# Matrix loads, slots' state, temperature constants and a planner's ranks rearranged in a fused attention and slot-GRU block

## The chip, the cores and the metric

The kernel runs on one core of a Trainium2 chip. The core has a matrix engine (TensorE, PE in the profile; its weight loads are listed as PEld), a vector engine (VectorE, DVE), a scalar engine (ScalarE, ACT), GpSimd (POOL) and SyncE (SP), which here only issues DMAs. Each engine works through its own queue of instructions in order and waits on semaphores for the others. The metric is the device time of one execution in microseconds, the median of several. Before the change it is 694.39 us (three runs, 693.93 to 694.57).

## What is computed

The input x is 32 sequences of 512 tokens of 256 floats. Two pre-normed blocks are added to it. The first is a causal attention within each sequence of 512 tokens, whose keys and queries are the same 64 features; the second routes each token to 64 slots, lets a GRU update the slots of each sequence, and reads them back. Everything is float32. The reference, cut:

```python
# first block, on the layer-normed x
q = tanh(x @ W_charge.T + b_charge)[..., 0]
phi_c = mags * q[..., None] ** arange(5)
shell = x @ W_shell.T + b_shell
shell = shell / maximum(norm(shell), 1e-12)
proj = shell @ omega.T + rff_bias
phi_s = concatenate([cos(proj), sin(proj)], -1) * rff_scale
phi = (phi_c[..., :, None] * phi_s[..., None, :]).reshape(b, n, -1) @ W_combine.T
T = exp(-0.3 * abs(idx[:, None] - idx[None, :]) / 10.0)
temp = softplus(log_temp) + 0.1
logits = where(causal, einsum('bnd,bmd->bnm', phi, phi) * T / temp, -inf)
out = softmax(logits) @ (x @ W_v.T + b_v) @ W_out.T + b_out
# second block, on the layer-normed sum
S = broadcast(slot_init * slot_scale)
h = gelu(concatenate([x, mean(S)], -1) @ w1.T + b1)
route = (h @ w2.T + b2) / (abs(tau) + 0.1)
alpha = softmax over the 8 largest of 64, zero elsewhere
gi = einsum('bts,btd->bsd', alpha, x) / alpha.sum(1)
gx, gh = gi @ gru_wih.T + gru_bih, S @ gru_whh.T + gru_bhh
h_new = GRU(gx, gh, S)
out = einsum('bts,bsd->btd', alpha, h_new @ wv.T + bv) @ wo.T + bo
```

The layer norms have no weights, so the kernel folds them: a centred weight matrix and one scale for each token.

## The kernel before

**Groups and stages.** The 32 sequences are taken two at a time: 16 groups of 1024 tokens (eight tiles of 128). Each group goes through the same stages, which are also the names in the planner's table `DELAY`. *load*: x, twice (once as it is, once by blocks for VectorE's transposes, from group 2 on). *tokens*: transposes of x (`pta`, line 907, by TensorE for groups 0 and 1, by VectorE, line 929, later), statistics `bna` (800) and their scale `lna` on POOL (811 to 817), the projection `pf` (959) to 321 columns, that is value, shell and charge, and its eviction `sv` by VectorE (972). *angles*: norms (`sq`, `rn`, `shn`), transposes (`ptq` 1018, `pts` 1089), the product with omega (`pp` 1106), sines, and the powers `tp` (1152). *phi*: `pph` (1164), evicted at 1179. *weights*: logits `pl` (1221), mask and maximum (1250), exponential `pr` (1262). *values*: transposes of the weights (`ptp` 1299, `prT` 1317), the product `po` (1305) and the addition to x (1334). *normal*: second layer norm (`lnb`, `xm`). *router*: a turn of xm through DRAM (`xd`, `xmb`; the last group turns it on TensorE), the hidden layer `ph` (1431), `prr` (1454), its transposes `prt` (1460), the eight largest (1485, 1486) and the softmax (1494 to 1519). *taken*: slot input `psi` (1543). *gru*: `prz`, `pn` (1596), `rz` (1609) and the gates. *given*: slot values `pv` (1684), read back by `py` (1704), addition (1718) and store (1723).

**Who sets the order.** Nothing is emitted where it is written. Each piece is a step of a `Plan` with an engine, a cost in microseconds, what it must follow and which buffers it uses. `Plan.order()` gives every step that has no rank of its own the rank: group times `STRIDE`, plus a mix (weighted by `LATE`) of its earliest start and its latest start within its group, plus the stage's `DELAY`; the second number of a `DELAY` counts for the last groups. It then places steps one at a time by start time and rank, with `HOP` for a hand-over between engines, `TABLE` for ScalarE's change of function table and `SWITCH` as a handicap on a TensorE step of another tile shape. The steps are emitted in the order of placement, which fixes each engine's queue. Setup steps carry written ranks: the lower, the earlier. DMAs from SP and ACT, and apart from these the ones from POOL, take completion semaphores in turn, eight of each kind.

**The setup that the change touches.** `value_and_out` (413) folds W_v and W_out into the projection: it loads both, centres W_v on VectorE (432 to 435), multiplies (`pw` 446), copies the product into `wf` (460), multiplies the bias (`pb` 478) and adds it into `bias_f` (491). A second call does the same for wv and wo of the slots (`wov`, `bias_s`). `wf` is centred by a mean product (`pm` 519, subtraction 525), then written to DRAM and read back by blocks as `wfb` (533 to 550), which groups 2 and up use. POOL makes `di`, the table of token distances, by three iotas (602 to 604); VectorE casts it (609); from it come `dec_k` (exponential) and `dec_q`, its four reciprocals (643) scaled by the temperature (628). The temperature and tau go through `scalars_1` (absolute values, exponential), `scalars_2`, a logarithm and `scalars_3` (614 to 628). The slots' state `hs` is loaded twice (for the two sequences of a group) with its scale `sc` (702 to 706) and multiplied. `whh` and the loads behind it feed the GRU's constant half (`pgh`, 744 to 780).

Scratch tiles of the setup stand in the five buffers of x: `setup_0` holds W_v and W_out, `setup_1` whh, `setup_2` wv and wo. Group 2's x takes the buffer of `setup_0` once the setup is done with it.

Of the kernel before, what the change touches and what calls it, by code (L numbers as in the profile page):

```python
# [11 lines left out]
AF = mybir.ActivationFunctionType  # L12
# [59 lines left out]
}  # L72


HOP = 0.21
TABLE = 1.28
SWITCH = 4.13
STRIDE = 29.1
LATE = 0.69

DELAY = {
    "setup": (0.0, 0.0),
    "load": (-39.8, 3.7),
    "tokens": (0.2, -3.0),
    "angles": (-18.5, -12.2),
    "phi": (8.4, 6.8),
    "weights": (14.1, -12.0),
    "values": (5.1, -15.9),
    "normal": (-0.8, 5.2),
    "router": (-1.4, -7.2),  # L90
    "taken": (1.6, -23.5),
    "gru": (16.3, 6.1),
    "given": (-12.8, -6.4),
}

SPARE = 3
# [149 lines left out]
def block_kernel(ctx: ExitStack, tc: tile.TileContext, a: dict, out: bass.AP):  # L246
# [163 lines left out]
        load("ACT", wf[:, :, 0:SHELL], rows(a["W_shell_t"]), 64, rank=-42.0, land=4.0),  # L410
    ]

    def value_and_out(wv_ap, bv_ap, wo_t_ap, bo_ap, w_dst, b_dst, n, centred, engs, rank):

        at = 2 * n
        wv = part(at, 0, [P, KD, D])
        wo_t = part(at, KD * D, [P, KD, D])
        bv_rep = part(at, 2 * KD * D, [P, KD, P])
        bo = part(at, 2 * KD * D + KD * P, [P, D])
        of = wv.of  # L420
        bv = const(f"bv{n}", [P, KD])
        mean = const(f"wv_mean{n}", [P, KD])
        land = 3.5 if centred else None
        l_wv = load(engs[0], wv, rows(wv_ap), 256, rank=rank, land=land)
        l_wo = load(engs[1], wo_t, rows(wo_t_ap), 256, rank=rank, land=land)
        l_bv = load(engs[2], bv, bv_ap.rearrange("(k p) -> p k", p=P), 8, rank=rank)
        l_bo = load(engs[2], bo, bo_ap.partition_broadcast(P), 128, rank=rank)
        last = l_wv
        if centred:

            def centre():
                nc.vector.tensor_reduce(mean, wv(), AX.X, ALU.add)
                nc.vector.tensor_scalar(mean, mean, 1.0 / D, None, ALU.mult)
                for k in range(KD):
                    nc.vector.tensor_scalar(
                        wv()[:, k, :], wv()[:, k, :], mean[:, k : k + 1], None, ALU.subtract
                    )

            last = add("DVE", 1.6, centre, [l_wv], of, rank=rank)
        done, made = [], []  # L440
        for m in range(KD):
            pw = bank(f"pw{n}_{m}")

            def project(m=m, pw=pw):
                for k in range(KD):
                    nc.tensor.matmul(
                        pw()[:, 0:D],
                        wv()[:, k, m * P : (m + 1) * P],
                        wo_t()[:, k, :],
                        start=(k == 0),  # L450
                        stop=(k == KD - 1),
                    )
# [13 lines left out]

        def spread():
            for k in range(KD):
                nc.vector.tensor_scalar(
                    bv_rep()[:, k, :], onesP, bv[:, k : k + 1], None, ALU.mult  # L470
                )

        s = add("DVE", 0.5, spread, [l_bv, s_ones], of, rank=rank)
        pb = bank(f"pb{n}")

        def project_bias():
            for k in range(KD):
                nc.tensor.matmul(
                    pb()[:, 0:D],
                    bv_rep()[:, k, :],  # L480
                    wo_t()[:, k, :],
                    start=(k == 0),
                    stop=(k == KD - 1),
                )

        s = add("PE", 1.6, project_bias, [s, l_wo], [pb] + of, rank=rank)
        done.append(
            add(
                "DVE",
                0.42,  # L490
                lambda: nc.vector.tensor_tensor(b_dst, pb()[:, 0:D], bo(), ALU.add),
                [s, l_bo],
                [pb] + of,
                rank=rank,
            )
        )
        return done, made
# [7 lines left out]
        bias_f[:, C_V:NF],  # L505
        0,
        True,
        ("SP", "ACT", "POOL"),
        -40.0,
    )  # L510
    l_bsh = [
# [21 lines left out]
    for q in range(P // SQ):  # L533
        for k in range(KD):
            kd, lo = divmod(q * KD * SQ + k * SQ, P)
            W_PFB.append(
                load(
                    "SP",
                    wfb[q * SQ : (q + 1) * SQ, k, :],
                    wf[lo : lo + SQ, kd, :],  # L540
                    40,
                    W_PF,
                    rank=2.0,
                    land=4.0,
                )
            )
# [66 lines left out]
    def scalars_1():  # L613
        nc.scalar.activation(sa, lt, AF.Abs)
        nc.scalar.activation(tau, tau, AF.Abs)
        nc.scalar.activation(sa, sa, AF.Exp, scale=-1.0)
        nc.scalar.activation(dec_k, df(), AF.Exp, scale=DECAY)

    def scalars_2():
        nc.vector.tensor_scalar(sa, sa, 1.0, None, ALU.add)  # L620
# [6 lines left out]
        nc.vector.reciprocal(rtemp, sb)  # L627
        nc.vector.tensor_scalar(dec_q, dec_q, rtemp, -1.0, ALU.mult, ALU.mult)

    s = add("ACT", 1.4, scalars_1, [l_lt, l_tau, s_df], df.of, table="exp", rank=4.0)  # L630
    s_exp = s
    s = add("DVE", 0.6, scalars_2, [s], rank=5.0)
    s_tau = s
    s = add("ACT", 1.5, lambda: nc.scalar.activation(sa, sa, AF.Ln), [s], table="ln", rank=5.0)
    s_sb = s

    def decays(after):

# [4 lines left out]
                lambda c=c: nc.vector.reciprocal(  # L643
                    dec_q[:, c * P : (c + 1) * P], dec_k[:, c * P : (c + 1) * P]
                ),
                [s_exp] + after,
                rank=9.0,
            )
            for c in range(NT)
        ]  # L650
        s_dec.append(add("DVE", 1.0, scalars_3, [s_sb] + s_rec, rank=10.0))

    s_dec = []


    def make_mask():
# [45 lines left out]
    l_hs = []  # L702
    for bb in range(GB):
        r = slice(bb * SLOTS, (bb + 1) * SLOTS)
        l_hs.append(load("SP", hs[r, :], a["slot_init"], 64, rank=31.0))
        l_hs.append(load("SP", sc[r, :], a["slot_scale"], 1, rank=31.0))
    s_hs = add(
        "DVE", 0.35, lambda: nc.vector.tensor_scalar(hs, hs, sc, None, ALU.mult), l_hs, rank=40.0
    )
# [33 lines left out]

    whh = part(1, 0, [P, KD, 3 * D])
    bih_rz = part(1, KD * 3 * D, [P, 2 * D])
    l_whh = load("SP", whh, rows(a["gru_whh_t"]), 768, rank=50.0)
    l_bih = [
        load("SP", bih_rz, a["gru_bih"][0 : 2 * D].partition_broadcast(P), 256, rank=51.0),
        load("SP", bih_n, a["gru_bih"][2 * D : 3 * D].partition_broadcast(P), 128, rank=51.0),
# [3 lines left out]
    for lo, n in ((0, 2 * D), (2 * D, D)):  # L753
# [26 lines left out]
        s = add("PE", 2 * n / 300.0, hidden, [s_hst, l_whh], [pg] + hs_t.of + whh.of, rank=70.0)  # L780
        W_GRU.append(add("DVE", 1.3, hidden_bias, [s, l_bhh] + l_bih, [pg, bhh] + whh.of, rank=71.0))
    s_wov, _ = value_and_out(
        a["wv"], a["bv"], a["wo_t"], a["bo"], wov, bias_s, 1, False, ("SP",) * 3, 72.0
    )


# [560 lines left out]
    def router(g, s_x, ln):  # L1347
# [134 lines left out]
        for t in range(GT):  # L1482
# [18 lines left out]
            "ACT",  # L1501
            0.68,
            lambda: nc.scalar.activation(rl(), rl(), AF.Exp, scale=rtau),
            [s, s_tau],
            [rl],
            "exp",
        )
# [225 lines left out]
    for g in range(NG):  # L1733
        plan.group = g
        plan.stage = "load"
        if g:

            if g == 1:
                load_x(g, rank=-30.0, lands=(8.5, 9.5))
            elif g == 2:  # L1740
                load_x(g, rank=0.0, lands=(6.0, 7.0))
            else:
                load_x(g, [l_w1s, l_whh])
        sv, s_sv, phi, s_phi = features(g)
# [66 lines left out]
```

## Time and profile before

The profiled execution took 696.3 us; the profile's span is 694.5 us, so 1.8 us lie around it. The mean granted clock of TensorE is 0.990 of full speed.

| | us | what it is |
|---|---|---|
| median of three runs | 694.39 | 693.93 to 694.57 |
| profiled execution | 696.3 | span 694.5 |
| first TensorE matmul (`pw`) | 10.78 | |
| first projection (`pf` of group 0) | 17.90 | TensorE was busy for 6.62 us until 17.40 |
| weights of group 0 (`pl`) | 48.95 | |
| projection of group 2 | 68.84 | |
| one group in the middle | 39.9 | `pf` of successive groups at 265.10, 305.00, 344.90, 384.80 |
| last `po` | ends near 641 | |
| last store | 694.5 | |

Times are read from the timeline of the trace. A group's "busy" is the time in which an engine runs an instruction; waits on semaphores are not in it. Where a row of the profile ends in brackets, it gives the idle time of the engine just before, and what ended it.

### The profile page before, as it was taken

To read this page: it belongs to the slowest core of one execution; us is meant where nothing else is said; L and a number is where in the kernel's file an instruction comes from. 1 tells how busy PE (TensorE), PEld (TensorE's weight loads), DVE (VectorE), ACT (ScalarE), POOL (GpSimd) and SP (SyncE) were. 2 spreads that over 40 slices of the span, in tenths; PEclk is the share of its full clock that TensorE was granted. 3 is DMA by queue.
4 is the path that set the end of the run, shared out by engine and by line. 5 is a ranking of instruction groups with operands and counts; after the bars stand their busy time and mean duration, and the time that the engine had idled before them with its cause. 6 is when DMAs were issued, how large, how long until landed. Compare 5 with 4: busy or idle time off the path is not lost.

```text
span 694.5 us, 12285 instructions
## 1 busy us (share of the span) xinstructions
PE 664.7 (96%) x3946; PEld 457.7 (66%) x3946; DVE 581.4 (84%) x1812; ACT 454.2 (65%) x1064; POOL 214.0 (31%) x400
## 2 busy tenths in 40 slices
PE   3979999999999999999999999999999999999885
PEld 3747666667666666767666666666766676678453
DVE  3987878799898989989897988989898968878586
ACT  1446676848585866758495775758676677486731
POOL 3550524133150613324061422406151233212200
PEclk9999999999999999999999999999999999999989
DMA  6672732445544444444535353543543433301004
GB/s 179 165 204 68 205 100 73 111 141 130 154 115 130 150 114 161 101 143 128 175 93 149 125 122 135 139 152 96 148 132 82 161 82 87 97 1 62 0 13 170
DMA packets 174255, 83.25 MB, mean 120 GB/s; under 512 B 123664, under 2 KB 173392, under 8 KB 174192
## 3 DMA queue, kind: packets, MB, share of 16 engines
q1 hardware_dynamic: 172880, 81.95, 41.8%
q8 instruction: 31, 0.51, 0.3%
q10 hardware_dynamic: 1104, 0.36, 0.2%
q0 software_dynamic: 208, 0.17, 0.2%
q14 instruction: 32, 0.26, 0.1%
HBM read 50.67 MB, written 31.46 MB: 118 GB/s over the span
## 4 chain that ended last, share of the span: by engine, by line
PE 89%; DVE 4%; DMA 2%; ACT 2%; issue 1%; POOL 0%; ACTq 0%; DVEq 0%; SPq 0%
PE po L1305 20%; PE pf L959 19%; PE ph L1431 7%; PE pl L1221 5%; PE pph L1164 5%; PE ptp L1299 5%; PE psi L1543 5%; PE py L1704 4%; PE prz L1596 4%; PE pn L1596 2%; PE pv L1684 2%; PE prr L1454 2%; PE pta L1667 1%; PE pp L1106 1%; DMA setup<-in_W_out_t_dram 1%; DMA wih<-in_gru_wih_t_dram 1%
## 5 line engine op out<-in xcount | busy, mean ns | idle before, releaser
L1305 PE MATMUL po<-sv,prT 128*128 128x256 f32 x640 | 151.7, 381 | 0.8 <-ACT prT L1317 0.8
L1305 PEld LDWEIGHTS po<-sv,prT 128*128 128x128 f32 x640 | 115.5, 189 | 24.2 <-issue 8.6
L959 PE MATMUL pf<-wfb,xT 128*128 128x321 f32 x448 | 125.6, 436 | 0.0
L959 PEld LDWEIGHTS pf<-wfb,xT 128*128 128x128 f32 x448 | 83.5, 189 | 39.7 <-DVE top L1485 3.5
L1371 ACT ACTIVATE xm<-x,lnb 128x256 f32<-128x256 f32 x128 | 63.9, 502 | 61.7 <-POOL lnb L1359 61.6
L1359 POOL TENSOR_SCALAR lnb<-lnb 128x2 f32<-128x2 f32 (+1 forms) x48 | 20.8, 434 | 266.7 <-DVE x L1334 264.4
L1334 DVE SCALAR_TENSOR_TENSOR x<-po,den,x 128x256 f32<-128x256 f32 x128 | 57.9, 479 | 27.1 <-PE po L1305 26.6
L1262 ACT ACTIVATE pr<-lg,nm 128x512 f32<-128x512 f32 (+3 forms) x128 | 70.8, 557 | 4.9 <-DVE nm L1250 4.0
L972 DVE SCALAR_TENSOR_TENSOR sv<-pf,lna,bias_f 128x321 f32<-128x321 f32 x128 | 64.7, 537 | 5.7 <-PE pf L959 5.1
L1401 ACT ACTIVATE xm<-x,lnb 128x256 f32<-128x256 f32 x112 | 56.9, 589 | 7.8 <-POOL lnb L1387 7.8
L1250 DVE CUSTOM_DVE_ANT_0 lg<-pl,mask 128x512 f32<-128x512 f32 (+3 forms) x128 | 55.6, 479 | 1.6 <-PE pl L1221 1.3
L1718 DVE TENSOR_TENSOR x<-py,x 128x512 f32<-128x512 f32 x64 | 39.8, 683 | 17.4 <-PE py L1704 17.3
L1431 PE MATMUL ph<-xmT,w1b 128*128 128x512 f32 x112 | 52.7, 594 | 0.0
L1317 ACT COPY prT<-ptp 128x384 f32<-128x384 f32 (+1 forms) x96 | 46.1, 516 | 5.4 <-PE ptp L1299 5.2
L800 DVE BATCH_NORM_STATS2 bna<-x 128x6 f32<-128x256 f32 x128 | 49.4, 413 | 0.0
L1299 PE MATMUL ptp<-ident,pr 128*128 128x128 f32 x320 | 45.8, 275 | 0.0
L1221 PE MATMUL pl<-phi 64*128 64x256 f32 (+1 forms) x384 | 43.8, 358 | 0.2 <-DVE phi L1179 0.2
L1299 PEld LDWEIGHTS ptp<-ident,pr 128*128 128x128 f32 x320 | 36.5, 141 | 9.3 <-issue 6.8
L1164 PE MATMUL pph<-tp,wc 64*64 64x256 f32 x640 | 39.8, 392 | 0.8 <-DVE tp L1152 0.8
L1152 DVE TENSOR_TENSOR tp<-tp,qs 128x1024 f32<-128x1024 f32 x32 | 38.7, 1211 | 2.1 <-ACT tp L1138 1.9
L1221 PEld LDWEIGHTS pl<-phi 64*128 64x128 f32 x384 | 30.5, 186 | 11.1 <-issue 7.2
L929 DVE STREAM_TRANSPOSE xT<-xb 128x512 f32<-128x512 f32 x56 | 36.6, 685 | 0.0
(174 smaller groups left out, 1241.6 us busy)
## 6 DMA issues: line engine op xcount, KB each, us to landing
x<-in_x_dram SPq DMA_DIRECT2D x32, 512.0 KB, 4.6
out_dram<-x SPq DMA_DIRECT2D x64, 256.0 KB, 2.5
xb<-in_x_dram SPq DMA_DIRECT2D x112, 128.0 KB, 2.8
xd<-xm SPq DMA_DIRECT2D x28, 512.0 KB, 2.9
xmb<-xd SPq DMA_DIRECT2D x112, 128.0 KB, 2.7
setup<-in_gru_whh_t_dram SPq DMA_DIRECT2D x1, 768.0 KB, 4.6
wih<-in_gru_wih_t_dram SPq DMA_DIRECT2D x1, 768.0 KB, 10.6
wfb<-wf SPq DMA_DIRECT2D x8, 40.1 KB, 3.4
```

The costliest lines, as they stand in the source:

```text
L959: nc.tensor.matmul(pf()[:, 0:NF], tile_()[:, k, c * P : (c + 1) * P], w[:, k, :], start=(k == 0), stop=(k == KD - 1),)
L972: lambda t=t, pf=pf: nc.vector.scalar_tensor_tensor(sv()[:, t, :], pf()[:, 0:NF], ln()[:, 1, t : t + 1], bias_f, ALU.mult, ALU.add,),
L1164: nc.tensor.matmul(phs[h]()[bb * COMB : (bb + 1) * COMB, 0:HT], wc[r, m, :], tp()[r, m, bb * HT : (bb + 1) * HT], start=(m == 0), stop=(m ...
L1221: nc.tensor.matmul(pls[bb]()[:, off[i] + lo : off[i] + lo + w], phi()[r, 0, q : q + P], phi()[r, 1, k : k + w], start=True, stop=True,)
L1250: nc.vector.tensor_tensor_reduce(out=lg()[:, c], in0=pls[bb]()[:, c], in1=mask[:, T - w : T], scale=1.0, scalar=TOP, op0=ALU.add, op1=ALU.min,
L1262: nc.scalar.activation(pr()[:, c], lg()[:, c], AF.Exp, bias=nm(), scale=-1.0, accum_out=den()[:, tiles.index(i), bb : bb + 1],)
L1299: nc.tensor.transpose(pt()[:, j : j + P], prs[bb]()[:, j : j + P], ident)
L1305: nc.tensor.matmul(po()[:, d * D : (d + 1) * D], pr_t()[:, lo : lo + P], sv()[:, bb * NT + j, C_V:NF], start=(j == 0), stop=(j == i),)
L1334: nc.vector.scalar_tensor_tensor(xt()[:, t, :], po()[:, d * D : (d + 1) * D], den()[:, d, bb : bb + 1], xt()[:, t, :], ALU.mult, ALU.add, ...
L1371: lambda bb=bb, i=i: nc.scalar.activation(xm()[:, bb * NT + i, 0:D], xt()[:, bb * NT + i, :], AF.Square, bias=ln()[:, 2, bb, i : i + 1], a ...
L1401: nc.scalar.activation(xm()[:, t, 0:D], xt()[:, t, :], AF.Identity, bias=bias, scale=scale)
L1431: nc.tensor.matmul(ph(), w1[:, k, :], dst()[:, k, :], start=(k == 0), stop=(k == KD - 1))
```

## The change

1. **Planner numbers.** `HOP` 0.21 to 0.29, `SWITCH` 4.13 to 0, `STRIDE` 29.1 to 22.7, `LATE` 0.69 to 0.98, and every `DELAY` but that of the setup. The order of all groups' steps on every engine is computed anew.
2. **W_out.** Its load goes from ACT's queue to SP's, right behind W_v. `value_and_out` takes a rank for the two matrices apart from that of their biases.
3. **Slots' state.** The four loads of `hs` and `sc` go from SP's queue to POOL's, behind those of bv, b_out and omega and ahead of the iotas.
4. **GRU and value matrices.** `whh`, `wv` and `wo` are issued on SP ahead of group 2's tokens, `wfb` and group 2's x later than before.
5. **Temperatures.** `scalars_1` no longer contains the exponential of `dec_k`, which stays early; the rest, with `scalars_2`, the logarithm and `scalars_3`, follows group 0's evictions.
6. **Reciprocals.** Each of the four reciprocals of `dec_k` follows one of group 0's last four evictions, instead of all four following all evictions.

```diff
-HOP = 0.21
+HOP = 0.29
-SWITCH = 4.13
-STRIDE = 29.1
-LATE = 0.69
+SWITCH = 0.0
+STRIDE = 22.7
+LATE = 0.98
-    "load": (-39.8, 3.7),
-    "tokens": (0.2, -3.0),
-    "angles": (-18.5, -12.2),
-    "phi": (8.4, 6.8),
-    "weights": (14.1, -12.0),
-    "values": (5.1, -15.9),
-    "normal": (-0.8, 5.2),
-    "router": (-1.4, -7.2),
-    "taken": (1.6, -23.5),
-    "gru": (16.3, 6.1),
-    "given": (-12.8, -6.4),
+    "load": (4.8, -12.9),
+    "tokens": (8.2, 7.0),
+    "angles": (-54.3, -7.8),
+    "phi": (-1.8, -10.7),
+    "weights": (11.9, 26.1),
+    "values": (9.7, -3.6),
+    "normal": (11.8, 2.3),
+    "router": (10.9, -19.7),
+    "taken": (-37.2, -20.0),
+    "gru": (-2.4, -1.6),
+    "given": (-3.5, 15.0),
...
-        land = 3.5 if centred else None
-        l_wv = load(engs[0], wv, rows(wv_ap), 256, rank=rank, land=land)
-        l_wo = load(engs[1], wo_t, rows(wo_t_ap), 256, rank=rank, land=land)
+        land = 3.3 if centred else None
+        first = rank if first is None else first
+        l_wv = load(engs[0], wv, rows(wv_ap), 256, rank=first, land=land)
+        l_wo = load(engs[1], wo_t, rows(wo_t_ap), 256, rank=first, land=land)
...
-        ("SP", "ACT", "POOL"),
+        ("SP", "SP", "POOL"),
...
-                    rank=2.0,
+                    rank=22.0,
...
-        nc.scalar.activation(dec_k, df(), AF.Exp, scale=DECAY)
...
-    s = add("ACT", 1.4, scalars_1, [l_lt, l_tau, s_df], df.of, table="exp", rank=4.0)
-    s_exp = s
-    s = add("DVE", 0.6, scalars_2, [s], rank=5.0)
-    s_tau = s
-    s = add("ACT", 1.5, lambda: nc.scalar.activation(sa, sa, AF.Ln), [s], table="ln", rank=5.0)
-    s_sb = s
+    s_exp = add(
+        "ACT",
+        0.7,
+        lambda: nc.scalar.activation(dec_k, df(), AF.Exp, scale=DECAY),
+        [s_df],
+        df.of,
+        table="exp",
+        rank=4.0,
+    )
...
-                [s_exp] + after,
-                rank=9.0,
+                [s_exp, after[4 + c]],
+                rank=-1.0,
...
-        s_dec.append(add("DVE", 1.0, scalars_3, [s_sb] + s_rec, rank=10.0))
+        s = add("ACT", 0.7, scalars_1, [l_lt, l_tau] + after, table="exp", rank=10.0)
+        s = add("DVE", 0.6, scalars_2, [s], rank=10.0)
+        s_tau.append(s)
+        s = add("ACT", 0.3, lambda: nc.scalar.activation(sa, sa, AF.Ln), [s], table="ln", rank=10.0)
+        s_dec.append(add("DVE", 1.0, scalars_3, [s] + s_rec, rank=10.0))
...
-        l_hs.append(load("SP", hs[r, :], a["slot_init"], 64, rank=31.0))
-        l_hs.append(load("SP", sc[r, :], a["slot_scale"], 1, rank=31.0))
+        l_hs.append(load("POOL", hs[r, :], a["slot_init"], 64, rank=-14.0))
+        l_hs.append(load("POOL", sc[r, :], a["slot_scale"], 1, rank=-14.0))
...
-    l_whh = load("SP", whh, rows(a["gru_whh_t"]), 768, rank=50.0)
+    l_whh = load("SP", whh, rows(a["gru_whh_t"]), 768, rank=-10.0)
...
-        a["wv"], a["bv"], a["wo_t"], a["bo"], wov, bias_s, 1, False, ("SP",) * 3, 72.0
+        a["wv"], a["bv"], a["wo_t"], a["bo"], wov, bias_s, 1, False, ("SP",) * 3, 72.0, -9.0
...
-                load_x(g, rank=0.0, lands=(6.0, 7.0))
+                load_x(g, rank=20.0, lands=(6.0, 7.0))
```

More of the change, by code (lines that the diff above doesn't have):

```diff
@@ L411, in block_kernel, with value_and_out @@
     ]
-    def value_and_out(wv_ap, bv_ap, wo_t_ap, bo_ap, w_dst, b_dst, n, centred, engs, rank):
+    def value_and_out(
+        wv_ap, bv_ap, wo_t_ap, bo_ap, w_dst, b_dst, n, centred, engs, rank, first=None
+    ):
         at = 2 * n
@@ L650, in decays @@
         ]
-        s_dec.append(add("DVE", 1.0, scalars_3, [s_sb] + s_rec, rank=10.0))
-    s_dec = []
+        s = add("ACT", 0.7, scalars_1, [l_lt, l_tau] + after, table="exp", rank=10.0)
[3 more added lines that the diff above has]
+        s_dec.append(add("DVE", 1.0, scalars_3, [s] + s_rec, rank=10.0))
+    s_dec, s_tau = [], []
     def make_mask():
@@ L1503, in router @@
             lambda: nc.scalar.activation(rl(), rl(), AF.Exp, scale=rtau),
-            [s, s_tau],
+            [s] + s_tau,
             [rl],
```

## The prediction

> **What bounds the kernel now.** I read the page's busy table first, then the slices, then the table by stretches, because a mean hides the ends.
>
> ```profile
> PE 664.7 (96%) x3946; PEld 457.7 (66%) x3946; DVE 581.4 (84%) x1812; ACT 454.2 (65%) x1064; POOL 214.0 (31%) x400
> ...
> PE   3979999999999999999999999999999999999885
> ...
> PE 89%; DVE 4%; DMA 2%; ACT 2%; issue 1%; POOL 0%; ACTq 0%; DVEq 0%; SPq 0%
> ```
>
> TensorE is busy 664.7 of 694.5 us and carries 89% of the chain that ended last. Outside the first and last slices there is nothing to win except by giving TensorE less to do. The stretches say the same in microseconds (columns: stretch, its length, then each engine's busy time, granted clock, DMA share, GB/s):
>
> ```profile
> 0.00:17.40 17.40, 6.62 (x28) 5.70 (x29) 6.44 (x19) 1.90 (x3) 6.88 (x22) 1.00 0.66 178
> 17.40:34.70 17.30, 17.30 (x82) 12.83 (x80) 16.08 (x47) 8.34 (x16) 9.74 (x22) 1.00 0.64 165
> 34.70:52.00 17.30, 13.14 (x109) 8.23 (x108) 15.46 (x35) 8.09 (x13) 8.84 (x15) 0.90 0.79 204
> ...
> 69.00:104.00 35.00, 33.63 (x197) 23.69 (x196) 28.91 (x83) 24.45 (x62) 13.02 (x29) 1.00 0.55 151
> 104.00:138.00 34.00, 33.11 (x176) 22.49 (x177) 27.01 (x90) 25.23 (x57) 9.34 (x15) 1.00 0.36 94
> ...
> 277.00:312.00 35.00, 35.00 (x212) 24.34 (x209) 30.55 (x98) 24.02 (x58) 11.25 (x20) 1.00 0.46 124
> ...
> 642.00:660.00 18.00, 15.95 (x59) 7.54 (x56) 9.17 (x37) 13.82 (x27) 3.90 (x6) 1.00 0.00 0
> 660.00:677.00 17.00, 15.08 (x79) 9.28 (x80) 13.88 (x48) 4.93 (x12) 0.00 (x0) 0.80 0.03 10
> 677.00:694.50 17.50, 9.34 (x52) 5.91 (x50) 10.71 (x22) 2.22 (x5) 0.00 (x0) 0.91 0.50 172
> ```
>
> TensorE's idle time is 10.8 us in the first stretch, 4.2 at 34.7 to 52, 2.3 from 69 to 138, none in the middle (35.00 of 35.00), and 2.1 + 1.9 + 8.2 in the tail. At 34.7 to 52 the clock is 0.90 too: it was halved from 42.77 to 46.20, after a thin stretch. The first wait, by the view of waits (total, times, longest):
>
> ```profile
> PE pw L446 <- DMA setup<-in_W_out_t_dram: 10.8, 1, 10.8
> ```
>
> The transfers of the start, by the view of DMA issues (the last column is us from issue to landing):
>
> ```profile
> setup<-in_W_v_dram SPq DMA_DIRECT2D x1, 256.0 KB, 3.5
> setup<-in_W_out_t_dram ACTq DMA_DIRECT2D x1, 256.0 KB, 8.9
> ...
> setup<-in_b_out_dram POOLq DMA_DIRECT2D x1, 128.0 KB, 7.9
> ...
> hs<-in_slot_init_dram SPq DMA_DIRECT2D x2, 64.0 KB, 2.4
> ...
> om<-in_omega_t_dram POOLq DMA_DIRECT2D x4, 8.0 KB, 8.0
> ```
>
> The same 256 KB took 3.5 us as the first on SP and 8.9 us on ACT's queue.
>
> **W_out on SP: what the first wait is worth.** Behind W_v (issued 0.73, landed 4.28) W_out should land near 5.5. VectorE centres W_v until 6.37, so pw can start at about 6.5 instead of 10.78. pw and pb take 5.3 us cold (3.75 + 1.5), so they end near 11.8. If nothing else held it, pf_0 (17.90, that is 7.1 us after pw) would start near 13.6: a gain of 4.3.
>
> **Slots' state on POOL's queue: what is late next.** POOL already issues bv, b_out and four om, by 5.24. Four more make ten, and in the changed kernel's built order the ninth and tenth carry a wait on the semaphores of bv and b_out: they are issued only when those have landed. b_out landed at 10.43. Behind those issues POOL has the three iotas of di (5.2 to 6.6 now, 2.1 us with gaps). So di would be ready at 10.4 + 2 = 12.4, and VectorE's cast of di stands ahead of both copies of pw in VectorE's order. It now comes early, by the timeline:
>
> ```profile
> 8.46 0.42 DVE L609 CAST setup<-di 128x512 f32<-128x512 int32 x1
> ```
>
> The copies, three statistics and bias_f behind it take about 3 us, to 15.8. Then come hs's scaling and only then wf's centring, which pf_0 needs; hs's scaling waits for the four landings. TensorE has pt_hs ahead of the second half of group 0's transposes, so it waits too.
>
> Here a rule stands against a row. The Trainium skill, "DMA: Bandwidth & Descriptors", section "Anatomy of one DMA — SWDGE (gpsimd) path", prices a transfer from GpSimd's queue at about 2.0 us plus its bytes at 436 KB/us, an estimate of 2.15 us for 64 KB and 2.3 for b_out. By it b_out lands at 4.9, nobody waits, di is ready near 8.5 and the gain is the 4.3. The rows say 7.9 for b_out and 8.0 for om at 8 KB, while the loads of x run. I take the row: hs issued near 8.5 and sc near 10.5 land at 14.8 to 16.5, wf is centred at about 16.6, and pf_0 starts at 17.4 (16.3 to 19). **Gain 0.5** (between -1.1 and 4.3). TensorE then has about 3 us of idling after pb, as long as the half-clock stretch that the trace shows at 42.77 to 46.20; one such stretch at half speed over the transposes costs **+0.8** (0 to 1.7).
>
> **GRU and value matrices ahead of x_2; wfb and x_2 late.** 768 + 512 KB go first. At the 165 to 204 GB/s of those stretches that is some 7 us of transfer, of which 2 to 3 delay xb_2 (to about 30); VectorE comes to group 2's transposes near 38. Hidden; if it were not, 2 us. In return pgh (1.9 + 0.9 us), pb1 (0.6) and pw1 (1.6) can stand in the gaps between group 0's angles and its weights. By pl_0 the changed order has done 3.7 us more (these, less pts_1 and pp_1), and at pf_2, which now starts at 68.84, 2.84 more. TensorE is idle 4.2 us at 34.7 to 52, but VectorE has 15.46 of 17.30 there and gets 1.65 us more ahead of phi_0. So about 3.0 of the idling is filled: **-3.0** (-3.5 to +1), of which 0.4 is given back in the stretch up to 69: **+0.4**.
>
> **Reciprocals and temperatures.** The four reciprocals (3.38 us in one piece at 27.23) go between the evictions of group 0: the same work. The last eviction is about 1.1 us later, and rn_0, which stood behind the four, is not. scalars_1 leaves dec_k's exponential and goes behind all evictions; scalars_2 and 3 with it. They are 0.14 to 0.5 us each. Rates for weights are needed only at pl_0 (48.95), and the chain Abs, Exp, Ln, reciprocal, scaling is 3 to 4 us with table loads of 1.28. Nothing, in the shadow of the angles; without it 1.3 for a table load.
>
> **New ranks.** HOP, SWITCH, STRIDE, LATE and all delays change, so the whole order changes. From 69 to 138 the angles get more room (ptq_1 had a wait of 2.56 for POOL's qrep, pts_2 0.94, ptq_2 0.89): 2.3 us were lost there and I take **-1.2** (-2.3 to 0). In the middle TensorE is full and can only lose. Before, groups 4 to 12 repeat one order; in the changed kernel each group's differs. Some producers stand closer to their users: pt_gi of group 11 has 0.3 us of other matmuls ahead of prz where VectorE or ScalarE must copy between them, pts_9 0.4, pv of groups 4 and 12 0.8 instead of 1.8, pph 1.3 to 2.3 ahead of pl instead of 8.8. No row shows those waits. Near rows are the short waits of 0.3 to 0.9 in the ramp; six to eight places lose part of that: **+1.0** (0 to 6).
>
> Matmuls of another tile shape follow each other more often: 215 changes of shape against 204. From the trace, a matmul of 256 columns starts 215 ns after one of the same shape and 306 to 309 ns after a change, so a change is worth 92 ns: 11 x 0.092 = **+1.0**. The Trainium skill, "TensorEngine Tiling (Array Packing)", section "Key Properties", says a mode switch drains the array; with the constant part of an isolated matmul from "TensorE: Matmul & The Clock Gate", "Single matmul latency", some 166 ns warm, it would be an estimate of 1.8. I take the row.
>
> **Tail.** In the changed order 3.2 us more of TensorE's work (prz_13, pn_13, pt_hn_13, one ptb_14) stands ahead of the last po_15, which ended near 641: **+3.2** at that point, and less is left behind it. What is left ran with waits:
>
> ```profile
> 657.69 1.28 ACT L1503 ACT_TABLE_LOAD   x1 [0.41 <-DVE rl L1494]
> ...
> 660.33 0.92 PE L1460 MATMUL prt<-ident,rlT 128*128 128x128 f32 x4 [2.23 <-ACT rlT L1468]
> ```
>
> prt_15 waits for ScalarE, which loaded a table for group 14's exponential first; with prt_14 ahead of the third transpose instead of behind it, that moves 0.65 earlier. py_13 (673.76 and 675.19) and VectorE's four adds of x_13 (674.93 to 677.65, ahead of rh at 677.56) stood between psi_15 and rz_15, and go in front: 1.7 to 1.9. Together **-2.5** (-4 to 0).
>
> **The sum**, against the profiled execution: -0.5 + 0.8 - 3.0 + 0.4 - 1.2 + 1.0 + 1.0 + 3.2 - 2.5 = -0.8. The profiled execution took 696.3 (span 694.5 and 1.8 around it); the median of the runs shown is 694.39, so I set the difference against that: **693.5 us**.
>
> **Rivals.** A, the start's gain is real: POOL's transfers are quicker when W_out no longer shares the time, or the semaphores do not hold di. For it: 2.4 us for the same hs on SP. Against: 6.4 to 8.0 for bv and om, the small transfers of POOL's queue. Then -4.3 in place of -0.5 + 0.8, partly absorbed by VectorE: about 689.5.
>
> B, slower: the irregular order stalls a full TensorE. Place: groups 3 to 13, at edges with less than about 1 us of other matmuls between a producer on TensorE and its next user. Price: a round trip by ScalarE or VectorE takes 1 to 2 us (copy 0.5 to 0.7 and two hand-overs), so 0.6 us a group, 11 groups, +6.6 in place of +1.0: about 699. It decides from 0.3 us a group on. For it: VectorE has 30.55 of 35.00 there, so it runs late easily. Against: only a few edges are that tight.
>
> C: the ramp gives nothing, since VectorE is full at 17 to 52 and phi_0 comes at 50 to 52 instead of 47.75, so the filled work only moves. -3.0 becomes 0: about 696.5.
>
> **How the numbers follow.** Forecast 0.40 (its own range 690.5 to 696.5), A 0.20, B 0.25, C 0.15. A measurement here cannot tell changes below 0.2%, or 1.4 us: 693.0 to 695.8. Of the forecast 0.17 lies below, 0.16 within, 0.07 above; A is 0.19 and 0.01; C 0.02, 0.04 and 0.09; B 0.02 within and 0.23 above. Faster 0.38, same 0.23, slower 0.39. The range leaves about a tenth out at either end: 688.5 to 700.
>
> **What would show it.** First matmul near 6.5; VectorE's cast of di near 12.4; pf_0 near 17.4 (A: below 15); the hs transfers 6 to 8 us from issue to landing (the page's price: about 2); pf_2 near 68 with pgh, pb1, pw1 done; TensorE 35.00 of 35.00 in the middle (B: 34.4); the last po near 641 with three steps of group 13 behind it; psi_15 to rz_15 below 5.3 us. The forecast is wrong if VectorE's work ahead of phi_0 sets the ramp or if the middle shows gaps.

## The result and the profile after

The changed kernel is slower: 705.51 us (703.63 to 705.76, four runs) against 694.48 us (693.93 to 696.22); the ratio is 1.0138, with an interval of 1.0107 to 1.0169. The forecast was 693.5. The profiled execution took 705.72 us, its span is 703.9 us, so 1.8 us lie around it as before. 9.4 us of span are to be found.

The page of the changed kernel: busy table, the slices of TensorE, the chain that ended last.

```profile
PE 672.5 (96%) x3946; PEld 458.8 (65%) x3946; DVE 578.7 (82%) x1812; ACT 461.2 (66%) x1071; POOL 212.0 (30%) x404
...
PE   3999999999999999999999999999899999999975
...
PE 82%; DVE 10%; ACT 3%; DMA 2%; issue 1%; POOL 1%; DVEq 0%; POOLq 0%; ACTq 0%; SPq 0%
```

TensorE's 3946 matmuls are the same, yet it is "busy" 7.8 us longer. The share is no help: 96% in both. The table by stretches (columns as in the prediction) shows where:

```profile
0.00:17.40 17.40, 6.31 (x26) 5.28 (x27) 5.99 (x18) 2.87 (x4) 8.90 (x26) 0.97 0.70 185
17.40:34.70 17.30, 17.30 (x70) 12.57 (x69) 14.38 (x43) 5.42 (x12) 6.87 (x15) 0.84 0.83 234
34.70:52.00 17.30, 15.65 (x101) 9.89 (x99) 16.21 (x37) 6.89 (x10) 9.71 (x23) 1.00 0.60 145
...
69.00:104.00 35.00, 35.00 (x228) 25.14 (x224) 27.60 (x78) 27.00 (x71) 13.48 (x28) 1.00 0.32 81
104.00:138.00 34.00, 34.00 (x214) 21.59 (x208) 26.93 (x89) 28.40 (x59) 5.92 (x11) 1.00 0.42 104
...
277.00:312.00 35.00, 35.00 (x213) 23.54 (x212) 29.50 (x91) 28.73 (x64) 11.87 (x21) 1.00 0.34 89
...
487.00:522.00 35.00, 33.09 (x188) 21.41 (x186) 26.39 (x79) 20.27 (x46) 7.53 (x13) 0.95 0.61 166
522.00:557.00 35.00, 34.76 (x197) 23.80 (x200) 29.54 (x94) 23.86 (x59) 11.34 (x21) 1.00 0.28 80
557.00:592.00 35.00, 33.81 (x228) 23.25 (x219) 29.46 (x85) 24.76 (x59) 11.68 (x23) 1.00 0.26 72
```

The last three stretches in the kernel before:

```profile
487.00:522.00 35.00, 35.00 (x210) 23.56 (x209) 31.09 (x100) 24.56 (x56) 12.83 (x23) 1.00 0.48 140
522.00:557.00 35.00, 35.00 (x218) 24.13 (x216) 30.86 (x93) 23.78 (x56) 7.66 (x12) 1.00 0.42 124
557.00:592.00 35.00, 35.00 (x196) 24.49 (x196) 26.85 (x88) 25.90 (x62) 13.95 (x26) 1.00 0.33 84
```

Four things are read here. The ramp did fill: 15.65 at 34.7 to 52 where 13.14 stood, and no idle time from 69 to 138 where 2.3 us were lost. The start is not earlier, and from 17.4 to 34.7 the clock is 0.84: TensorE is busy all of the 17.30 us and does 70 matmuls instead of 82. The middle still says 35.00 of 35.00, and the longest wait of TensorE between 185 and 425 us is 0.5 us. From 487 us on, where the kernel before had 35.00 in each stretch up to 592, TensorE waits and once runs slowly.

A busy share can't show what a stretch at 35.00 achieved. So each matmul is given the duration that its kind takes when nothing holds it (start to start, from the kernel before: 215 ns for 256 columns, 269 for 321, and so on; 602 us for all), and the table compares when the two kernels come to the same amount of this work. It holds microseconds behind (+) or ahead (-) of the kernel before, from one profiled execution each; the experiments below are added. At 560 the last `po` ends 10 to 14 us later.

| work done, us | 0 | 40 | 120 | 240 | 320 | 440 | 480 | 520 | 560 | 602 |
|---|---|---|---|---|---|---|---|---|---|---|
| time before, us | 11 | 63 | 151 | 283 | 370 | 500 | 544 | 586 | 631 | 688 |
| changed kernel | -5.0 | -0.4 | -2.6 | -0.8 | +0.7 | +1.2 | +5.3 | +8.4 | +7.9 | +9.7 |
| after_again | -5.0 | -2.2 | -4.4 | -2.5 | -1.0 | -0.6 | +2.0 | +5.0 | +4.6 | +6.4 |
| ramp_of_after | -5.1 | -1.9 | -4.1 | -3.2 | -3.2 | -3.2 | -3.2 | -3.2 | -3.2 | -3.5 |
| tail_of_before | -5.0 | -2.0 | -4.2 | -2.4 | -0.9 | +0.7 | +0.7 | +0.7 | +0.7 | +0.3 |
| wout_alone | -5.2 | -4.3 | -4.3 | -4.3 | -4.3 | -4.3 | -4.3 | -4.3 | -4.3 | -6.0 |
| after_hs_late | -4.7 | -4.1 | -6.4 | -4.5 | -3.0 | -2.5 | +1.6 | +4.7 | +4.2 | +5.1 |
| after_gelu_first | -5.1 | -0.9 | -3.1 | -1.2 | +0.3 | +0.7 | +1.1 | +4.2 | +3.7 | +4.6 |
| both_ramp_and_order | -4.4 | -4.1 | -6.3 | -5.4 | -5.4 | -5.4 | -5.4 | -5.4 | -5.4 | -7.2 |
| gate_bias_later | -4.4 | -5.2 | -7.4 | -6.5 | -6.5 | -6.5 | -6.5 | -6.5 | -6.5 | -6.5 |

So the changed kernel is 2.6 us ahead at 150 us, gives 3.8 back over 350 us of full TensorE, loses 4.1 around one place near 505 us, and the rest from there to the end. The row after_again is a second profiled execution of the same kernel; the two differ where the clock was slow, and elsewhere by 0.1 us at most.

**The place near 505 us.** First TensorE's timeline of the changed kernel, then ScalarE's (columns: start, duration, engine, line, operation, output and input; in brackets the idle time before and what ended it):

```profile
500.26 3.70 PE L1440 MATMUL ph<-xmT,w1b 128*128 128x512 f32 x8
503.80 1.25 PE L968 MATMUL pf<-wfb,xT 128*128 128x321 f32 x4
506.95 1.74 PE L968 MATMUL pf<-wfb,xT 128*128 128x321 f32 x4 [1.91 <-ACT h_t L1449]
508.62 3.63 PE L1173 MATMUL pph<-tp,wc 64*64 64x256 f32 x40
```

```profile
500.86 4.04 ACT L1410 ACTIVATE xm<-x,lnb 128x256 f32<-128x256 f32 x8 [0.40 <-POOL lnb L1396]
504.92 1.28 ACT L1449 ACT_TABLE_LOAD   x1
506.21 1.27 ACT L1449 ACTIVATE h_t<-ph,b1e 128x512 f32<-128x512 f32 x2
```

The projection of group 13 waits 1.9 us for a bank of PSUM, where the kernel has TensorE put its products. The bank is held by the hidden layer `ph` of group 10 until ScalarE's gelu (`h_t`) has read it, and in the new order that gelu and its table load stand behind eight `xm` of group 11. Then comes a second price: from 507.77 to 511.19 the granted clock is half, and the 40 `pph` take 3.63 us; elsewhere they take 2.39.

**The start.** POOL's and VectorE's timelines:

```profile
5.20 0.56 POOL L280 DMA_DIRECT2D hs<-in_slot_init_dram  x1
5.72 0.56 POOL L280 DMA_DIRECT2D sc<-in_slot_scale_dram  x1
8.73 0.53 POOL L280 DMA_DIRECT2D hs<-in_slot_init_dram  x1 [2.45 <-DMA bv<-in_b_v_dram]
11.03 0.52 POOL L280 DMA_DIRECT2D sc<-in_slot_scale_dram  x1 [1.77 <-DMA setup<-in_b_out_dram]
```

```profile
12.85 0.83 DVE L612 CAST setup<-di 128x512 f32<-128x512 int32 x1 [3.81 <-POOL di L607]
...
16.58 0.35 DVE L717 TENSOR_SCALAR hs<-hs,sc 128x256 f32<-128x256 f32 x1 [0.61 <-issue]
```

The two waits on POOL's queue are there, the cast of di comes at 12.85 (12.4 was foretold), and the scaling of the slots' state at 16.58, since the last `sc` landed at 16.50. `pw` begins at 5.78, but `pt_hs` at 16.99 after 5.3 us of waiting. Then the clock is half from 16.25 to 23.08, and the first projection begins at 19.18.

### The profile page after: what moved, and what is told of

Same layout as the page of the kernel before. It is cut to its first block, busy times and chain, and to the rows that moved or that the text cites. A ratio compares the mean times of both kernels' runs of the same rounds, so it can differ in the third digit from the quotient of the medians.

```text
span 703.9 us, 12286 instructions
## 1 busy us (share of the span) xinstructions
PE 672.5 (96%) x3946; PEld 458.8 (65%) x3946; DVE 578.7 (82%) x1812; ACT 461.2 (66%) x1071; POOL 212.0 (30%) x404
## 4 chain that ended last, share of the span: by engine, by line
PE 82%; DVE 10%; ACT 3%; DMA 2%; issue 1%; POOL 1%; DVEq 0%; POOLq 0%; ACTq 0%; SPq 0%
PE po L1314 19%; PE pf L968 16%; PE ph L1440 7%; PE pl L1230 5%; PE pph L1173 5%; PE ptp L1308 5%; PE psi L1552 4%; PE py L1713 4%; PE prz L1605 4%; PE prr L1463 2%; PE pv L1693 2%; PE pn L1605 2%; DVE rest L1495 2%; PE pp L1115 1%; DVE sv L981 1%
## 5 line engine op out<-in xcount | busy, mean ns | idle before, releaser
L968 PE MATMUL pf<-wfb,xT 128*128 128x321 f32 x448 | 131.0, 438 | 1.9 <-ACT h_t L1449 1.9
L1259 DVE CUSTOM_DVE_ANT_0 lg<-pl,mask 128x128 f32<-128x128 f32 (+3 forms) x128 | 56.6, 481 | 10.1 <-PE pl L1230 9.8
L1054 POOL TENSOR_TENSOR sq<-sv 128x256 f32<-128x256 f32 x32 | 20.0, 626 | 128.0 <-DVE sv L981 121.2
L1308 PE MATMUL ptp<-ident,pr 128*128 128x128 f32 x320 | 47.7, 276 | 0.9 <-ACT pr L1271 0.5
L1230 PE MATMUL pl<-phi 64*128 64x256 f32 (+1 forms) x384 | 45.8, 362 | 1.7 <-DVE phi L1188 1.5
L809 DVE BATCH_NORM_STATS2 bna<-x 128x6 f32<-128x256 f32 x128 | 46.3, 409 | 0.0
L1368 POOL TENSOR_SCALAR lnb<-lnb 128x2 f32<-128x2 f32 (+1 forms) x48 | 13.3, 279 | 100.7 <-DVE x L1343 94.3
```

The source lines that it names most:

```text
L968: nc.tensor.matmul(pf()[:, 0:NF], tile_()[:, k, c * P : (c + 1) * P], w[:, k, :], start=(k == 0), stop=(k == KD - 1),)
L1230: nc.tensor.matmul(pls[bb]()[:, off[i] + lo : off[i] + lo + w], phi()[r, 0, q : q + P], phi()[r, 1, k : k + w], start=True, stop=True,)
L1259: nc.vector.tensor_tensor_reduce(out=lg()[:, c], in0=pls[bb]()[:, c], in1=mask[:, T - w : T], scale=1.0, scalar=TOP, op0=ALU.add, op1=ALU.min,
L1308: nc.tensor.transpose(pt()[:, j : j + P], prs[bb]()[:, j : j + P], ident)
```

## Experiments

All ratios are to the kernel before on the same chip.

**Numbers alone, edits alone, slots' state back, no late numbers.** These four let the planner plan anew.

numbers_only: in the kernel before,

```diff
-HOP = 0.21
+HOP = 0.29
...
-    "load": (-39.8, 3.7),
+    "load": (4.8, -12.9),
...
```

> The kernel before with the new HOP, SWITCH, STRIDE, LATE and DELAY alone, and none of the edits to the setup. Theory (the planner's numbers cost the time behind the ramp): the 12.7 us that the changed kernel lost from about 105 us on come here too, without the ramp's gain of 3 us: 707 us (703 to 709). Rival (the edits to the setup cost it): about 694.

Measured 718.59 us, ratio 1.0336 (1.0301 to 1.0370).

edits_only: the same block of numbers put back in the changed kernel.

> The changed kernel with the old HOP, SWITCH, STRIDE, LATE and DELAY: only the edits to the setup. Theory: the ramp's gain of about 3 us stays and nothing is lost behind it: 691.4 us (690 to 694.4). Rival (the edits cost the time): about 705. Second rival (the ramp's gain needs the new numbers): 694.4 or a little more, since the slots' state still holds the first projection back.

Measured 743.29 us, ratio 1.0689 (1.0661 to 1.0717).

after_hs_sp: in the changed kernel,

```diff
-        l_hs.append(load("POOL", hs[r, :], a["slot_init"], 64, rank=-14.0))
-        l_hs.append(load("POOL", sc[r, :], a["slot_scale"], 1, rank=-14.0))
+        l_hs.append(load("SP", hs[r, :], a["slot_init"], 64, rank=31.0))
+        l_hs.append(load("SP", sc[r, :], a["slot_scale"], 1, rank=31.0))
```

> The changed kernel with the slots' state back on SP's queue (rank 31, as before). Theory: the first projection starts at 14 to 15 us instead of 19.18, and the half-clock stretch behind it goes; the 5 us are kept to the end: 700.5 us (699 to 703). Rival (VectorE absorbs the start's gain before the weights of group 0): 704 to 706.

Measured 720.70 us, ratio 1.0370 (1.0338 to 1.0401).

no_late: in the changed kernel every second number of `DELAY` is 0.

> The changed kernel with the second number of every DELAY at 0: the order is that of the changed kernel up to group 12, and new behind it. Theory (the late numbers make the stall at 504.6 us and what follows, 8.7 us in all): 2 to 5 us of the 8.7 remain, 699 to 702 us. Rival (the stall comes from the first numbers, since it stands at the first projection of group 13, or the tail needs late numbers of some kind): 705 or more.

Measured 733.94 us, ratio 1.0562 (1.0534 to 1.0589). The stall near 505 stayed, as the rival said (5.8 us behind at 480 of work done), and the tail became 28 us worse.

No theory foretold that all four would be slower than both kernels. So the loss can't be put down to the numbers or to the edits by such runs: any change to either gives other orders for all groups, and all four new orders were worse. (That each set of numbers had been fitted to its own setup would explain this, but is not shown.) Everything below, but wout_replanned, therefore keeps an order and changes a few steps in it.

**Two orders joined.** The group steps are the same in both kernels. In the changed kernel, what is left behind a cut is emitted in the order of the kernel before:

```diff
-        for s in plan.order():
+    placed = plan.order()
+    done = placed[:CUT]
+    byn = {at[id(s)]: s for s in placed[CUT:]}
+    placed = done + [byn[n] for n in OTHER if n in byn]
...
+        for s in placed:
             s.emit()
```

ramp_of_after has CUT = 849.

> No planning anew: the changed kernel's steps in the changed kernel's order up to group 4's features (about 185 us), then all that is left in the order of the kernel before. Theory (the changed kernel gains about 2 us up to there and loses 12 behind it, by the order alone): 692.5 us (691 to 694.5), as the kernel before from there on. Rival (what follows the edits loses whatever its order): 700 or more.

Measured 693.47 us, ratio 0.9972 (0.9961 to 0.9982): 1.9 us faster than before.

tail_of_before has CUT = 1915.

> The changed kernel's order up to group 10's angles (about 425 us), then the order of the kernel before for all that is left. Theory (the loss of 9 us behind 490 us is one of the order of the last groups): 695.2 us (694 to 697.5). Rival (it comes from lateness that has built up by then on VectorE and ScalarE): 701 or more.

Measured 697.38 us, ratio 1.0032 (1.0021 to 1.0044): 2.2 us slower than before. The stretches of tail_of_before where the changed kernel stalled:

```profile
487.00:522.00 35.00, 35.00 (x212) 23.89 (x210) 31.42 (x98) 24.57 (x55) 12.43 (x23) 1.00 0.49 141
522.00:557.00 35.00, 35.00 (x214) 24.15 (x214) 30.51 (x94) 23.77 (x57) 8.04 (x13) 1.00 0.42 125
```

TensorE is full again. The runs give the change in three parts: -1.9 up to 185 us, 2.2 + 1.9 = +4.1 from there to 425, and what is left of the whole behind it. The whole was 9.6 us (1.38% of 694.5) in the first measurement and, in a second one further below, 7.2; so +5 to +7.4. All of the loss is thus in the order of the steps behind 185 us: both joined kernels contain every edit to the setup.

**The stall near 505 us.** after_gelu_first keeps the changed kernel's order but for two steps of ScalarE:

```diff
+    gelus = [s for s in placed if s.eng == "ACT" and s.table == "gelu" and s.g == 10]
+    normed = [s for s in placed if s.eng == "ACT" and s.stage == "normal" and s.g == 11 and s.cost == 0.51]
+    move(gelus, normed[2])
```

> The changed kernel in its own order, but on ScalarE group 10's two gelus stand behind the second of the eight xm of group 11 instead of behind the last. Theory (TensorE's stall of 1.9 us at 505 us is the wait for the bank that the gelu frees, and the half-clock stretch behind it follows from it): no stall there, no half clock at 507.8 to 511.2, 3.6 us less: 702 us (700.5 to 703.5). Rival (the xm that come later hold the next hidden layer back, or VectorE is as late): 705.

Measured 701.23 us, ratio 1.0086 (1.0071 to 1.0102), and the timelines of TensorE and ScalarE:

```profile
503.39 2.33 PE L968 MATMUL pf<-wfb,xT 128*128 128x321 f32 x8
505.64 2.39 PE L1173 MATMUL pph<-tp,wc 64*64 64x256 f32 x40
```

```profile
500.45 1.09 ACT L1410 ACTIVATE xm<-x,lnb 128x256 f32<-128x256 f32 x2 [0.40 <-POOL lnb L1396]
501.56 1.28 ACT L1449 ACT_TABLE_LOAD   x1
502.86 1.42 ACT L1449 ACTIVATE h_t<-ph,b1e 128x512 f32<-128x512 f32 x2
504.17 3.05 ACT L1410 ACTIVATE xm<-x,lnb 128x256 f32<-128x256 f32 x6
```

Two steps moved, and the eight projections run without a gap, `pph` at full clock; the later `xm` cost nothing. Against the first measurement of the changed kernel that is 3.6 us (1.0138 less 1.0086, of 694.5), as expected. Against the second it is 1.2, and there the intervals overlap. The trace of after_again says why: the gap of 1.9 us is there, but `pph` behind it runs at full clock (2.39 us). In the table the way from 440 to 480 costs 0.4 us here, against 4.1 and 2.6 in the two executions of the changed kernel. The gap is the order's; the slow stretch behind it comes in some executions only.

**The start.** after_hs_late keeps the order and takes the slots' state out of the way: SP issues the four loads ahead of whh, and the scaling, transposes and mean go behind the first evictions.

```diff
+        l_hs[-1].emit = lambda r=r: nc.sync.dma_start(out=hs[r, :], in_=a["slot_init"])
...
+    move(l_hs, l_whh)
+    move([s_hs], sv_of[0][6])
+    move([s_pth], first["pe1"][0])
+    move([s_hst], first["pe1"][3])
```

> The changed kernel in its own order, but the slots' state is loaded by SP ahead of whh, and its scaling, transposes and mean stand behind group 0's projection; POOL's iotas come at once. Theory: pf of group 0 at 13.6 to 15 us instead of 19.18, no half-clock stretch there, and 5 us kept of it: 700.5 us (699 to 702.5). Rival (VectorE takes the gain back): 705.

Measured 701.35 us, ratio 1.0083 (1.0062 to 1.0105): 3.8 us less than the first measurement of the changed kernel, 1.4 less than the second, where the intervals overlap. TensorE's timeline:

```profile
6.04 3.71 PE L449 MATMUL pw<-setup 128*128 128x256 f32 x8 [6.04 <-DVE setup L438]
...
12.79 8.82 PE L970 MATMUL pf<-wf,xT 128*128 128x321 f32 x32
```

The first projection comes at 12.79 instead of 19.18 and takes 8.82 us instead of 10.76. Of the 6.4 us at the first projection 3.7 are left at 40 of work done. The next loss is in the timelines of VectorE and TensorE:

```profile
43.71 0.69 DVE L784 TENSOR_TENSOR gh_rz<-pgh,bhh 128x512 f32<-128x512 f32 x1 [1.65 <-DMA bhh<-in_gru_bhh_dram]
...
45.65 0.41 DVE L1190 TENSOR_TENSOR phi<-pph,dec_q 128x256 f32<-128x256 f32 x1
```

```profile
46.77 2.83 PE L1232 MATMUL pl<-phi 64*128 64x256 f32 x11 [2.58 <-DVE phi L1190]
```

VectorE stands at the GRU's bias sum, ahead of phi, until bhh lands: a wait that no longer fits, since bhh is loaded as late as ever. TensorE pays 2.58 us, and from 47.08 to 50.50 half clock.

after_kept_busy asks what the slow clock alone costs. It leaves all waits and gives TensorE work to do in them:

```diff
     def hs_transposed():
+        for _ in range(46):
+            nc.tensor.transpose(pt_hs()[:, KD * P : (KD + 1) * P], onesD, ident)
```

> The changed kernel with 46 transposes of a constant by TensorE ahead of pt_hs, into columns that nobody reads: TensorE is busy from 11.7 to 16.7 us, where it waited. Theory (the half clock at 16.25 to 23.08 is the consequence of that wait and costs 3 us): no half clock there, pf of group 0 at 18.2 instead of 19.18 and 2 to 3 us less at the end, 703 us. Rival (VectorE, whose first eviction waits for POOL until 21.85, hides the slow clock): 705.

Measured 702.83 us, ratio 1.0115 (1.0096 to 1.0133). TensorE's timeline:

```profile
12.05 5.18 PE L724 MATMUL pt_hs<-ident,onesD 128*128 128x128 f32 x46
17.08 0.38 PE L726 MATMUL pt_hs<-ident,hs 128*128 128x128 f32 x2
...
18.17 8.82 PE L970 MATMUL pf<-wf,xT 128*128 128x321 f32 x32
```

The slow clock goes, and the projection takes 8.82 us. But the intervals of the two ratios overlap. So both kernels were run once more, unchanged, on one chip.

> The changed kernel once more, for the size of the change beside the other runs: 1.0138, that is 704.5 to 705.5 us. If the half clock at the start costs 2 us or more, after_kept_busy lies 2 us or more below it.

> The kernel of after_kept_busy once more, on the chip of after_again. Theory (the half clock at the start costs 2 to 3 us): 702 to 703 us. Rival (hidden by VectorE): within 1 us of after_again.

Measured 702.31 us (701.33 to 705.69), ratio 1.0103 (1.0076 to 1.0129), and 702.64 us (701.88 to 703.74), ratio 1.0098 (1.0078 to 1.0118). The gain of 2 to 3 us that I expected is not there; the rival's "within 1 us" holds, though not shown for its reason, that VectorE hides the slow clock. The granted clock shows another: the start's slow stretch lasted 6.83 us in the first profiled execution of the changed kernel (16.25 to 23.08) and 3.41 in the second (16.23 to 19.64), and the one near 508 us was absent from the second. Two stretches of 3.41 us at half speed less are 3.4 us, and the spans are 703.9 and 700.6. The six times of after_again fall into two heaps, 701.3 to 702.4 and 705.4 to 705.7.

**W_out alone, without and with the planner.** In the kernel before, in its own order:

```diff
+            wo_load.append(l_wo)
+            l_wo.emit = lambda: nc.sync.dma_start(out=wo_t(), in_=rows(wo_t_ap))
...
+    move(wo_load, x_in[0][0])
```

> The kernel before in its own order, with the load of W_out issued by SP behind W_v instead of by ACT, and nothing else. Theory (di is early here, so the first wait's removal reaches the first projection): pf of group 0 at 13.6 to 14.5 us instead of 17.9, and 690 to 693 us. Rival (VectorE, nearly full up to group 0's weights, takes the gain back): 694.4.

Measured 691.86 us, ratio 0.9950 (0.9932 to 0.9969). `pw` starts at 5.63 and the first projection at 12.79. Of the 4.3 us ahead at 40 of work done nothing is lost to the end; the last 1.7 go with a slow stretch of the tail (660.6 to 667.4 in the kernel before) that this execution did not have.

wout_replanned makes the same edit where the planner sees it:

```diff
-        ("SP", "ACT", "POOL"),
+        ("SP", "SP", "POOL"),
```

> The kernel before with W_out on SP as in wout_alone, but given to the planner, which then sets another order for all groups. Theory (each set of numbers fits one setup, and any change of it re-plans for the worse): 2 to 20 us above wout_alone, 694 to 712. Rival (the planner copes, and the loss lies in the new numbers as such): 691 to 693.

Measured 755.20 us, ratio 1.0861 (1.0840 to 1.0881), worse than any value expected. The same transfer from the same queue is 3.5 us faster or 60 us slower, by the order alone. Five times, some 90 us apart, TensorE waits 4.7 us for one exponential behind another, which is 23 of the 60 us:

```profile
193.41 0.93 PE L1221 MATMUL pl<-phi 64*128 64x128 f32 x8
199.00 1.11 PE L1299 MATMUL ptp<-ident,pr 128*128 128x128 f32 x4 [4.67 <-ACT pr L1262]
```

**Ramp and order together.** both_ramp_and_order is after_hs_late up to CUT = 849, then the order of the kernel before.

> The changed kernel's ramp with the slots' state late and on SP (as in the run after_hs_late), then from group 4's features on the order of the kernel before. Theory (ramp and order are separate): 6 us ahead of the kernel before at 185 us and to the end, 688.5 us (687 to 690.5). Rival (W_out on SP alone has all that the ramp can give): 691 to 692, as the run wout_alone.

Measured 690.74 us, ratio 0.9934 (0.9911 to 0.9958), just above the range expected. It is 5.4 us ahead instead of 6 from group 4's features on, and the interval overlaps that of wout_alone.

gate_bias_later is the same with VectorE's bias sums out of the way, since the wait for bhh was still there:

```diff
+    firsts = [s for s in placed if s.eng == "DVE" and s.stage == "weights" and s.g == 0]
+    move(bias_steps, firsts[0])
+    if placed.index(x_in[3][0]) < placed.index(firsts[0]):
+        move(x_in[3], firsts[1])
```

> As both_ramp_and_order, but VectorE's two additions of the GRU's biases (gh_rz, gh_n) stand behind group 0's phi instead of ahead of it. In after_hs_late VectorE waits 1.65 us there for bhh to land and TensorE 2.58 us for phi, with half clock behind it. Theory (that wait is where the earlier start is lost): TensorE's wait for phi below 1 us, no half clock at 47 us, 2 to 3 us less than both_ramp_and_order: 688 us (686.5 to 689.5). Rival (VectorE's work ahead of phi is the limit, not the wait): 690 to 691.

Measured 689.25 us, ratio 0.9909 (0.9884 to 0.9934). TensorE's timeline where it waited 2.58 us for phi:

```profile
44.33 1.03 PE L584 MATMUL pw<-setup 128*128 128x256 f32 x4
45.30 2.12 PE L1369 MATMUL pl<-phi 64*128 64x256 f32 x16
```

The wait is gone and no half clock follows; 6.5 us ahead from 240 of work done to the end. It is the fastest of all, 0.9% below the kernel before; by how much it beats both_ramp_and_order and wout_alone is not shown, since the intervals overlap.

## Why the prediction was wrong

- **The first wait**: right. `pw` at 5.78 (6.5 foretold), W_out landed at 5.64.
- **Slots' state ahead of di**: right in mechanism and nearly in time: the cast of di at 12.85, the scaling at 16.58, landings 5.5 to 8.5 us after issue. The row of the profile was the better guide than the 2.15 us estimated from the Trainium skill, "DMA: Bandwidth & Descriptors", section "Anatomy of one DMA — SWDGE (gpsimd) path": the two transfers of `hs` took 8.5 and 6.4. That this edit swallowed the gain is shown by after_hs_late and wout_alone, both with the first projection at 12.79. Rival A's size was real, but not for this kernel.
- **"One such stretch at half speed ... +0.8 (0 to 1.7)"**: a fair price for one stretch; the kernel had two in a row at the start in one profiled execution, one in the other. `pf_0` came at 19.18 instead of 17.4. Right ahead of it stand `pt_hs` and eight transposes: 2.2 us at half clock, and 1.1 at full clock in after_kept_busy, where it came at 18.17. So about 1.1 of the 1.8 us is the clock.
- **Start, filling and angles together**: -3.5 foretold; -2.6 and -4.4 at 120 of work done in the two executions. This is partly luck: up to 40 of work done -2.3 was foretold and -0.4 and -2.2 came, while the angles behind it gave 2.2 in both instead of 1.2. (Of the waits that the prediction lists there, `ptq_1`'s 2.56 ended at 41.58 and belongs to the 4.2 us at 34.7 to 52; the 2.3 us from 69 to 138 are right without it.) Rival C, that the filling gives nothing, does not hold: the first projection comes 1.3 us later than before, and at 40 of work done the kernel is 0.4 and 2.2 us ahead.
- **"Six to eight places lose part of that: +1.0 (0 to 6)"**: the step that failed. It took short waits from the ramp as the measure, at edges between two steps of TensorE. With +1.0 for changes of tile shape, 2.0 us were allowed between the ramp and the last `po`; from 120 to 560 of work done the two executions lost 10.5 and 9.0. Of these 3.8 are spread over 350 us in both, the kind of loss that the step meant, though more. The rest, 5.2 to 6.7, lies in the last groups, from 490 us on, where the prediction weighed only how close a step of TensorE stands to the next one that needs its result. The largest single stall was not an edge between two TensorE steps at all: it was a bank held by a queue on ScalarE (1.9 us, and up to 1.7 more by the clock), and after_gelu_first removes it. To foresee it one has to ask, for each PSUM bank, what stands ahead of its last reader on that reader's engine.
- **Changes of tile shape, +1.0**: the count is right (215 against 204), the price too low. The 92 ns are what a change away from the full 128x128 tile costs; the traces have 93 for it between 120 and 440 of work done. A change back costs 198 to 252 there, counted against the spacing within a run of the smaller tile (107 or 54 ns). The average is 0.17 us, and by it the term is an estimated 1.8.
- **The tail**: right in size, in part by luck. 3.2 us more of work are ahead of the end of the last `po` (571.7 against 568.5). Behind it the way to the end takes 51.5 us against 53.6, which is 2.1 less where 2.5 less was forecast. From the end of `psi_15` to `rz_15` it is 3.6 us instead of 5.0, most of the 1.7 to 1.9 foretold. But some 0.8 us is the clock, for which the forecast had no term: `psi_14` took 3.70 us before and 2.91 after.
- **Rival B** (699) had the sign and the kind, a full TensorE stalled by the new order, but spread it evenly at 0.6 a group; over half came behind 490 us.
- **The sum**: -0.8 from 694.39 gives 693.6, not 693.5; this changes nothing.

Open: which edges make the 4 us between 185 and 425, and what is left of the last groups once the gelu is moved (3.5 us in the table from 480 to the end). No run took these apart. The traces give a part of the first: between 120 and 440 of work done TensorE's order has 7 more changes of tile shape of some 120, and the time at them is an estimated 1.0 to 1.3 us more; the waits that the profile shows there come to 0.8 us.

## What to carry to other kernels

When an edit is to be judged in a kernel whose order comes from a planner, keep the order and change a few steps in it, or planning anew hides the effect: here an edit worth 3.5 us became one that cost 60. Where an engine is full, look for the buffers that it waits to get back, and at what their last reader does first. A resource moved off a queue is moved onto another: the loads that left SP held up POOL's next work, because the transfers ahead of them had to land first.

## What was not expected of the hardware

Half clock came in stretches of 3.41 us or twice that (3.42 at 507.77, 6.83 at 16.25, 3.41 at 16.23), beginning after a wait of 1.9 us or more and reaching into the work that follows. The same wait of 1.9 us, in the same kernel, was followed by such a stretch in one profiled execution and not in the other. The traces show what differed. In each of the two, the slow stretches begin on a raster of 3.413 us (507.77 - 16.25 is 144 times that). In the first execution the wait lay within one cell of the raster: TensorE was busy for 1.50 us from 504.36 to 507.77, and the next cell was slow. In the second the work came 1.7 us earlier, by the shorter slow stretch at the start, and the same wait fell into two cells, with 2.39 us busy from 500.92 to 504.34 and 2.53 from there to 507.75; no slow one followed. This is read from two traces; no run moved a wait within a cell to test it. Each slow stretch of 3.41 us costs up to 1.7 us, so two executions of one order can differ by 3.4 us, a third of the change under study, and a difference of that size between single profiles has to be looked up in the granted clock first.
